# Moving a bias to VectorE, holding fillers behind two norms, and re-timing the gathers of a graph network kernel

## The chip, the cores and the metric

The kernel runs on one core of one Trainium2 chip. A core has five engines that run side by side, each with its own queue of instructions: TensorE (PE in the profile, its weight loads PEld), VectorE (DVE), ScalarE (ACT), GpSimd (POOL) and SyncE (SP, which here only issues DMAs). The metric is the device time of one execution in microseconds; the median of several executions counts.

## The reference

A graph of 2500 nodes with 256 features and 40000 edges goes through two layers, each with a residual. Cut to what matters:

```python
xn = layernorm(x)
x = x + graph_mean(xn) @ W_l.T + xn @ W_r.T + b_r + linear_attention(xn)   # no softmax
x = x + experts(layernorm(x))                    # top 2 of 8, hidden 512
xn = layernorm(x)
x = x + gcn(xn) + transformer(xn)                # 2 aggregations; 4 layers of attention + MLP
x = x + experts1(layernorm(x))                   # shared hidden 1024, best 1 of 8
```

`graph_mean` sums `xn[src]` per `dst` and divides by the count. `gcn` aggregates twice, each time `segment_sum(h[src] * norm, dst) + b` over the edges and a loop on each node, with a leaky rectifier between. One layer of `transformer` is `x += attention(norm(x)); x += gelu(norm(x) @ W1 + b1) @ W2 + b2`, with 256 to 1024 to 256, and attention with a softmax over the features of a query and over the nodes for a key.

## The kernel before

Nodes lie on 125 partitions in 20 tiles (`NT`), worked on in 5 groups (`NG`) of 4 tiles (`GT`, 500 nodes). `X` holds the residual, `Y` the transformer's own. Everything is in fp32, but the one-hots, the adjacency and three bf16 parts of `xn`.

The stages in time: an input stage that finds each node's edges and computes the first attention's 256 x 256 matrix from the Gram matrix of `xn` (to about 81 us); the dense adjacency, built from one-hots, and its product with `xn` (to about 335); the first experts (to about 575); four transformer layers with the two aggregations of `gcn` gathered beside them (to 1711); and the last experts.

*Order.* A framework traces the Python program and plans the order of each engine's instructions by a cost model: an instruction that is planned as ready may be issued ahead of one that stands before it in the program, as a filler. `with tc.issue_after(ins):` keeps what is traced inside it, on the engine of `ins`, behind `ins` in that engine's queue. It adds no wait.

*Input stage.* `norm_stats` (L437 to L440) gives mean and variance, `rsqrt` (L406 to L413) the roots in a dozen small VectorE steps. Groups 0 and 1 are normed first, then 2 to 4; `less` (L756) is the last step of each, and ACT then writes the rows (L763). PE transposes them (L457) and adds up the Gram matrix `pgm` (L769). `count_edges` (L225 to L247) counts edges per node on VectorE and sends the counts through DRAM on SP; `split3` (L447 to L450) splits the rows into three bf16 parts `xb`. Both come after the Gram chain in the program. After them five GpSimd additions put the bias `b0` on `X` (L817), one for each group.

*Adjacency.* `build_tile` makes one-hots `ohd` and `ohs` on VectorE (L151), PE multiplies them (L837), ACT casts the result into `edges` (L840). `neighbours` multiplies `xb` with a group's `edges` (L398); then VectorE adds the two products to `X` (L880, L881). Four tiles are built ahead of the first group.

*Transformer layers.* `attention(l)`: five groups are normed and turned, keys (L1257) follow with their maxima `kmax` (L1259), `top` (L1269, L1270) and the exponentials (L1274); `pk` (L1289) multiplies the transposed keys (L1284, copied by ACT at L1286) with the rows; `context_out` copies it (L1176, L1177). Then come scores of queries by pairs of tiles (`scores`: L1303, L1308 to L1315), their transposes (`turn`: L1321), products (`attend`: L1330) and the addition to `Y` (L1333). `norm_rows(0)` and `norm_turn(0)` norm group 0 for the feed-forward part: `less` (L467), ACT (L469), PE (L457), ACT (L462). `ffn` runs 5 groups with 8 hidden products (L1365, gelu at L1368), 4 times 8 output products (L1376), and an addition (L1378); between them it steps the next groups' attention by a table written by hand.

*Gathers.* The 2000 and more nodes outside group 0 are ranked by degree into 16 ranks of 128. `gathers` fetches for each rank the node's own row and then its neighbours' rows with GpSimd indirect DMAs (L1076), four to a piece, 4 pieces ahead; VectorE adds each piece (L1088; L1092 and L1094 at a rank's end). Round 1 finishes a rank with `rectified` (ACT at L1107 into `b`, VectorE at L1108 to L1111) and scatters it (L1098); round 2 reads that table. Group 0 is multiplied densely instead (`dense`, L1044, finished by `first_group`). Where the adds stand in the program is set by a plan in us: each piece is due at `GATHER` times the gathers before it, counted from the round's beginning, and `conv_step(now)`, called at 88 places of a layer, runs what is due:

```python
while under and under[0][1] + under[0][2] + LANDING <= now:
    run, _, begun = under.pop(0)
    with tc.issue_after(last["add"]):
        passed = next(run, None)
```

`now` is `LAYER * l` plus a share of `AHEAD` in the head of a layer (keys from -0.6 of it, `pk` to 0.7, scores to 0.95), and in `ffn`:

```python
conv_step(LAYER * l + AHEAD + (LAYER - 1.6 * AHEAD) * (g + step / (nj + GT)) / NG)
```

`last["add"]` is the VectorE instruction behind which the adds are queued.

Of the kernel before, what the change touches and what calls it, by code (L numbers as in the profile page):

```python
# [9 lines left out]
F32 = mybir.dt.float32  # L10
# [3 lines left out]
ALU = mybir.AluOpType  # L14
# [4 lines left out]
D = 256  # L19
P = 125  # L20
NT = N // P
GT = 4
NG = NT // GT
# [12 lines left out]
NR = len(MOST)  # L36
SUM = 4
LEAD = 4
GATHER = 1.27
LANDING = 12.0  # L40
LAYER = 237.0
AHEAD = 40.0
NBIN = 64
NE = 8
F0 = 512
# [15 lines left out]
def gps_kernel(ctx: ExitStack, tc: tile.TileContext, a, out):  # L61
# [46 lines left out]
    X = whole[:P]  # L108
# [336 lines left out]
    def split3(dst, src, eng=V):  # L445

        S.copy(dst[:, :, 0, :], src)  # L447
        eng.tensor_tensor(src, src, dst[:, :, 0, :], ALU.subtract)
        S.copy(dst[:, :, 1, :], src)
        eng.tensor_tensor(dst[:, :, 2, :], src, dst[:, :, 1, :], ALU.subtract)  # L450
# [13 lines left out]
    def normal_rows(rows, src, lo, mv, rstd):  # L464

        less = small.tile([P, GT], F32, tag="less", name="less")
        V.scalar_tensor_tensor(less, mv[:, :, 0], -1.0, rstd, ALU.mult, ALU.mult)  # L467
        for k in range(GT):
            S.activation(rows[:, k, :D], src[:, lo + k, :D], AF.Identity, bias=less[:, k:k + 1], scale=rstd[:, k:k + 1])  # L469

    def layernorm_T(src, dst, keep, gain=None, shift=None, stats=None, then=None):

# [254 lines left out]
    with tc.tile_pool(name="lay0", bufs=1) as lay0:  # L727
# [9 lines left out]
        with tc.tile_pool(name="gram", bufs=1) as gram:  # L737
            wk, wv, wfc, wq = (
                load_w(gram.tile([128, 2 * D], F32, name=name[-3:]), a[name], D)
                for name in ("L0_mix_WkT", "L0_mix_WvT", "L0_mix_WfcT", "L0_mix_Wq")  # L740
            )
            bq = gram.tile([128, 2], F32, name="bq")
            nc.sync.dma_start(bq, a["L0_mix_bq"])
            bvc = gram.tile([128, 2], F32, name="bvc")
            nc.sync.dma_start(bvc, a["L0_mix_bv"].rearrange("o (c p) -> p (o c)", p=128))
            bkv = gram.tile([128, 2 * D], F32, name="bkv")
            nc.sync.dma_start(bkv[:, 0:D], row_bcast(a["L0_mix_bk"], 0, D, 128))
            nc.sync.dma_start(bkv[:, D:2 * D], row_bcast(a["L0_mix_bv"], 0, D, 128))


            pgm = [psum2.tile([128, D + 1], F32, tag="ag", name=f"pgm{c}") for c in range(2)]
            rows = []
            for lo, n in ((0, 2 * GT), (2 * GT, NT - 2 * GT)):
                mv, rstd = norm_stats(X, lo, n)
                less = gram.tile([P, n], F32, name="less")
                V.scalar_tensor_tensor(less, mv[:, :, 0], -1.0, rstd, ALU.mult, ALU.mult)  # L756
                for g in range(lo // GT, (lo + n) // GT):
                    t = gram.tile([P, GT, D + 1], F32, tag="t", name="t", bufs=NG)
                    G.memset(t[:, :, D:D + 1], 1.0)
                    rows.append(t)  # L760
                    for k in range(GT):
                        i = g * GT + k
                        S.activation(t[:, k, :D], X[:, i, :D], AF.Identity, bias=less[:, i - lo:i - lo + 1],  # L763
                                     scale=rstd[:, i - lo:i - lo + 1])
                    transpose_group(xT, g, lambda k: t[:, k, :D])
                    for k in range(GT):
                        i = g * GT + k
                        for c in range(2):
                            T.matmul(pgm[c], t[:, k, c * 128:(c + 1) * 128], t[:, k, :], start=(i == 0), stop=(i == NT - 1))  # L769


            gr = gram.tile([128, 2, D + 1], F32, name="gr")
            for c in range(2):
                V.tensor_copy(gr[:, c, :], pgm[c])
            xv = gram.tile([128, 2, D], F32, name="xv")
            for c in range(2):
                ps = mm_tile(128, D)
                for kc in range(2):
                    T.matmul(ps, gr[:, kc, c * 128:(c + 1) * 128], wv[:, kc, :], start=(kc == 0), stop=(kc == 1))
                V.scalar_tensor_tensor(xv[:, c, :], bkv[:, D:2 * D], gr[:, c, D:D + 1], ps, ALU.mult, ALU.add)  # L780
            sv = gram.tile([128, 2], F32, name="sv")
            for c in range(2):
                ps = mm_tile(128, 1)
                for kc in range(2):
                    T.matmul(ps, wv[:, kc, c * 128:(c + 1) * 128], gr[:, kc, D:D + 1], start=(kc == 0), stop=(kc == 1))
                V.scalar_tensor_tensor(sv[:, c:c + 1], bvc[:, c:c + 1], float(N), ps, ALU.mult, ALU.add)
            gm = gram.tile([128, 2, D], F32, name="gm")
            for h in range(2):
                ps = mm_tile(128, 128)
                for kc in range(2):  # L790
                    T.matmul(ps, xv[:, kc, h * 128:(h + 1) * 128], wk[:, kc, h * 128:(h + 1) * 128],
                             start=(kc == 0), stop=(kc == 1))
                cm = gram.tile([128, 128], F32, tag="cm", name="cm", bufs=2)
                V.scalar_tensor_tensor(cm, bkv[:, h * 128:(h + 1) * 128], sv[:, h:h + 1], ps, ALU.mult, ALU.add)
                V.scalar_tensor_tensor(cm, cm, 1.0 / N, heads, ALU.mult, ALU.mult)
                pm = mm_tile(128, D)
                T.matmul(pm, cm, wfc[:, h, :], start=True, stop=True)
                V.tensor_copy(gm[:, h, :], pm)

            for c in range(2):  # L800
                ps = mm_tile(128, D)
                for h in range(2):
                    T.matmul(ps, wq[:, h, c * 128:(c + 1) * 128], gm[:, h, :], start=(h == 0), stop=(h == 1))
                V.tensor_tensor(wx[:, c, :], wx[:, c, :], ps, ALU.add)
            lost = count_edges(gram)
            for g in range(NG):
                split3(xb[:, g * GT:(g + 1) * GT], rows[g][:, :, :D])
            bqs = gram.tile([128, 2, P], F32, name="bqs")
            V.tensor_copy(bqs, bq[:, :, None].to_broadcast([128, 2, P]))
            ps = mm_tile(P, D)  # L810
            for h in range(2):
                T.matmul(ps, bqs[:, h, :], gm[:, h, :], start=(h == 0), stop=(h == 1))
            V.tensor_tensor(b0[:, 0, :], b0[:, 0, :], ps, ALU.add)

        for g in range(NG):
            o = X[:, g * GT:(g + 1) * GT, :D]
            G.tensor_tensor(o, o, b0[:, 0, None, :].to_broadcast([P, GT, D]), ALU.add)  # L817

        degrees(cnt[:, 0:NT])
        rval = small.tile([P, NT], F32, tag="rval", name="rval")  # L820
# [4 lines left out]
        with tc.tile_pool(name="build", bufs=1) as build:  # L825
# [20 lines left out]
            for g in range(NG):  # L846
# [23 lines left out]
                aT = build.tile([128, 2, GC], F32, tag="aT", name="aT", bufs=2)  # L870
                for c in range(2):
                    (S.copy if c else V.tensor_copy)(aT[:, c, :], pa[c])
                for k in range(GT):
                    i = g * GT + k
                    ps = mm_tile(P, 2 * D)
                    for c in range(2):
                        T.matmul(ps[:, :D], xT[:, c, i * P:(i + 1) * P], wx[:, c, :], start=(c == 0), stop=(c == 1))
                    for c in range(2):
                        T.matmul(ps[:, D:], aT[:, c, k * P:(k + 1) * P], wl[:, c, :], start=(c == 0), stop=(c == 1))
                    V.tensor_tensor(X[:, i, :D], X[:, i, :D], ps[:, :D], ALU.add)  # L880
                    V.scalar_tensor_tensor(X[:, i, :D], ps[:, D:], rval[:, i:i + 1], X[:, i, :D], ALU.mult, ALU.add)  # L881
# [107 lines left out]
    with tc.tile_pool(name="big", bufs=4) as big, tc.tile_pool(name="hid", bufs=8) as hid, \  # L989
# [113 lines left out]
        def rectified(o, ps, by, by2):  # L1103

            n = o.shape[0]
            b = conv.tile([128, D], F32, tag="b", name="b")[:n]
            S.activation(b, b1row[:n], AF.Identity, scale=by)  # L1107
            V.scalar_tensor_tensor(o, ps, by2, b, ALU.mult, ALU.add)  # L1108
            neg = conv.tile([128, D], F32, tag="neg", name="neg")[:n]
            V.tensor_scalar(neg, o, 0.0, alpha[:n], ALU.min, ALU.mult)  # L1110
            V.scalar_tensor_tensor(o, o, 0.0, neg, ALU.max, ALU.add)  # L1111
# [103 lines left out]
        def attention(l):  # L1215
# [123 lines left out]

            def norm_rows(g):  # L1340
                mv, rstd = norm_stats(Y, g * GT, GT)
                normal_rows(rows2[:, g * GT:(g + 1) * GT, :], Y, g * GT, mv, rstd)

            def norm_turn(g):
                transpose_group(fT, g, lambda k: rows2[:, g * GT + k, :D], g1[:, 2, :], g1[:, 3, :])
# [43 lines left out]
            def step_scores(u):  # L1389
                qs_of[u] = scores(u)  # L1390
# [7 lines left out]
            for u in range(2):  # L1398
                step_turn(u)
                step_attend(u)  # L1400
            norm_rows(0)
            for u in range(2):
                step_scores(u + 2)
                conv_step(LAYER * l + AHEAD * (0.85 + 0.1 * u))
            norm_turn(0)
            for _ in range(2):
# [316 lines left out]
```

## Time and profile before

| what | value |
|---|---|
| median of 3 runs | 2059.2 us (2053.08 to 2060.47) |
| profiled execution, its own time | 2055.05 us |
| its span, first to last instruction | 2053.4 us |
| mean granted TensorE clock | 0.938 |
| busy: PE, DVE, POOL, ACT | 1777.1, 1006.6, 903.6, 667.8 us |
| indirect DMAs for the gathers (L1076) | 590.7 us busy in its largest group, 1029 ns each |
| adds of pieces (L1088) | 145.9 us busy, 1128 ns each |

A line of the timeline or of a group reads: start and duration in us (in a timeline), engine, source line, operation, what is written and read by the program's names, shapes, the number of instructions merged, and in brackets the engine's idle time before it with what ended it. A line of the waits reads: who waited, for whom, us in total, times, longest. A wait costs time only where the waiting engine is the one that everything else waits for. In the stretches, a pair such as 38.08 (x166) is us busy and instructions, and the clock is a share of full speed.

### The profile page before, as it was taken

The page shows a single profiled execution, that of the slowest core. Times are in us where ns is not written, and L with a number is a line of the kernel's source. Part 1 is how long each engine was busy: PE and PEld are TensorE (multiplying, and loading weights), DVE is VectorE, ACT ScalarE, POOL GpSimd, SP SyncE. Part 2 cuts the span into 40 slices and gives each one's busy share as a digit, 9 for nine tenths or more (in the row PEclk, how much of TensorE's full clock was granted, in tenths as well). Part 3 has the DMA queues.
Part 4 walks back from the last instruction along what each step waited for, and adds up shares of the span by engine and source line. Part 5 has one row for each costly group of instructions (what it writes and reads, how often), then busy time and mean ns, then how long its engine had stood idle before and what let it go on. Part 6 is the DMA issues. An engine that isn't in the chain of part 4 may idle for free. (4 is left out here: it accounts for less than half of the span.)

```text
span 2053.4 us, 24869 instructions
## 1 busy us (share of the span) xinstructions
PE 1777.1 (87%) x8153; PEld 1264.5 (62%) x8153; DVE 1006.6 (49%) x2948; ACT 667.8 (33%) x1228; POOL 903.6 (44%) x898
## 2 busy tenths in 40 slices
PE   2799891999868799997899977998989998976997
PEld 2556551888747567665566655775666766435665
DVE  7867633333362456643567425556444536223333
ACT  1553210322244133442344432434423330442220
POOL 2402632342204567775575575777764310132222
PEclk9799995999979899999999988999999999997999
DMA  5030115675444633373233574456732111511100
GB/s 127 2 98 22 22 29 170 211 234 179 130 128 123 122 80 96 112 206 113 64 96 89 147 131 128 139 154 182 204 109 67 38 41 62 155 38 30 34 21 23
DMA packets 122772, 213.26 MB, mean 104 GB/s; under 512 B 28889, under 2 KB 86881, under 8 KB 122378
## 3 DMA queue, kind: packets, MB, share of 16 engines
q0 software_dynamic: 45632, 105.31, 19.7%
q1 hardware_dynamic: 72181, 98.21, 15.7%
q10 hardware_dynamic: 4821, 8.04, 1.5%
q8 instruction: 70, 1.15, 0.2%
q14 instruction: 68, 0.56, 0.1%
HBM read 172.08 MB, written 41.42 MB: 104 GB/s over the span
## 5 line engine op out<-in xcount | busy, mean ns | idle before, releaser
L1076 POOL DMA_INDIRECT piece<-tab,nbr x574 | 590.7, 1029 | 269.5 <-issue 153.9
L1376 PE MATMUL mm<-w,h 128*125 128x256 f32 x1280 | 290.4, 381 | 5.7 <-ACT h L1368 5.5
L1365 PE MATMUL mm<-xT,w 128*128 128x500 f32 x640 | 290.9, 598 | 2.6 <-ACT xT L462 2.6
L1376 PEld LDWEIGHTS mm<-w,h 128*125 128x125 f32 x1280 | 239.0, 189 | 50.2 <-issue 9.2
L1365 PEld LDWEIGHTS mm<-xT,w 128*128 128x128 f32 x640 | 122.3, 196 | 119.6 <-issue 107.9
L1088 DVE TENSOR_TENSOR piece<-piece 128x1024 f32<-128x1024 f32 (+3 forms) x130 | 145.9, 1128 | 85.8 <-DMA piece<-tab,nbr 85.3
L1368 ACT ACTIVATE h<-mm,bf 128x500 f32<-128x500 f32 x160 | 106.8, 675 | 201.9 <-PE mm L1365 201.7
L398 PE MATMUL pa<-edges,xb 125*128 125x500 bf16 x600 | 137.2, 382 | 1.7 <-ACT edges L840 1.7
L965 POOL DMA_INDIRECT back<-yo,idx x47 | 46.1, 981 | 148.8 <-DVE idx L951 76.6
L1628 PE MATMUL py<-wd,taken 128*128 x432 | 98.6, 386 | 10.4 <-DVE taken L1618 10.4
L457 PE MATMUL mm<-ident,tok 125*128 125x125 f32 x360 | 55.8, 293 | 57.3 <-ACT tok L469 36.4
L945 PE MATMUL mm<-xc,wt 128*128 128x128 f32 x752 | 97.0, 283 | 7.0 <-DVE idx L951 4.2
L521 POOL DMA_INDIRECT sorted<-rows,to x40 | 49.2, 1229 | 121.0 <-DVE to L516 89.4
L1378 DVE TENSOR_TENSOR tok<-tok,mm 125x256 f32<-125x256 f32 x80 | 33.5, 418 | 138.5 <-PE mm L1376 138.4
L945 PEld LDWEIGHTS mm<-xc,wt 128*128 128x128 f32 x752 | 89.8, 195 | 17.1 <-DVE xc L941 11.6
L959 PE MATMUL py<-w,h 128*128 x376 | 97.7, 386 | 2.1 <-ACT h L949 2.0
L1333 DVE TENSOR_TENSOR tok<-tok,po 125x256 f32<-125x256 f32 x80 | 30.0, 417 | 141.3 <-PE po L1330 141.2
L398 PEld LDWEIGHTS <-xb 125*128 125x128 bf16 x600 | 58.8, 101 | 65.3 <-issue 6.8
L1628 PEld LDWEIGHTS py<-wd,taken 128*128 128x128 f32 x432 | 82.5, 193 | 25.9 <-DVE taken L1618 13.4
L949 ACT ACTIVATE h<-mm,wt 128x128 f32<-128x128 f32 x188 | 53.7, 368 | 136.7 <-issue 127.3
L1289 PE MATMUL pk<-kt,tok 125*128 125x256 f32 x320 | 80.3, 402 | 18.4 <-ACT kt L1286 16.8
L840 ACT CAST edges<-mm 125x500 bf16<-125x500 f32 x100 | 64.6, 783 | 82.9 <-PE mm L837 82.9
(407 smaller groups left out, 3041.5 us busy)
## 6 DMA issues: line engine op xcount, KB each, us to landing
wt<-in_expert_in_dram SPq DMA_DIRECT2D x47, 514.0 KB
sorted<-nothing SPq DMA_DIRECT2D x5, 2031.2 KB
piece<-tab,nbr POOLq DMA_INDIRECT x574, 3.1
e<-adj SPq DMA_DIRECT2D x40, 218.8 KB
w<-in_L_mix_W_dram SPq DMA_DIRECT2D x8, 1024.0 KB
wd<-in_L_ffn_Wd_dram SPq DMA_DIRECT2D x8, 1024.0 KB
xs<-sorted SPq DMA_DIRECT2D x47, 130.0 KB
t<-tab SPq DMA_DIRECT2D x20, 224.0 KB
```

The source lines that it names most:

```text
L398: T.matmul(pa[c], table[:, k, n, c * 128:(c + 1) * 128], edges[:, k, :], start=(k == 0 and n == 0), stop=(k == NT - 1 and n == 2))
L457: T.transpose(ps[:, k * P:(k + 1) * P], src_of(k)[:, c * 128:(c + 1) * 128], ident[:P, :P])
L840: S.copy(o.rearrange("p s (n d) -> p n s d", d=BD), ps[:P].rearrange("p (n s d) -> p n s d", n=BD, d=BD))
L945: T.matmul(ps[:, j * TS:(j + 1) * TS], wt[:, c * F0 + j * 128:c * F0 + (j + 1) * 128], xc[:, c * TS:(c + 1) * TS], start=(c == 0), stop=(c ...
L959: T.matmul(ps, h[:, j * TS:(j + 1) * TS], w2[:, ds(e, 1), j, :], start=(j == 0), stop=(j == NJ - 1))
L1076: G.indirect_dma_start(out=t[:, i, :], out_offset=None, in_=tab, in_offset=bass.IndirectOffsetOnAxis(ap=by, axis=0))
L1088: V.tensor_tensor(total[:, :m, :], total[:, :m, :], t[:, :m, :], ALU.add)
L1289: T.matmul(pk[c], rows[:, i, c * 128:(c + 1) * 128], kt, start=(i == 0), stop=(i == NT - 1))
L1365: T.matmul(ps, w1[:, c, j * 128:(j + 1) * 128], fT[:, c, g * GC:(g + 1) * GC], start=(c == 0), stop=(c == 1))
L1368: S.activation(h, ps, AF.Gelu, bias=bf[:, l, j:j + 1])
L1376: last["product"] = T.matmul(ps, hh[j][:, k * P:(k + 1) * P], w2[:, j, :], start=(j == 0), stop=(j == nj - 1)).ins
L1628: T.matmul(ps, h[:, j * TS:(j + 1) * TS], wd[:, ds(e, 1), j, :], start=(j == 0), stop=(j == nj - 1))
```

## The change

Five edits. The first layer's bias is added on VectorE, for one group at a time, inside the loop over groups, just before the products of that group are added. `count_edges` and `split3` are queued, on VectorE, behind the `less` of the second norm (the loop's variable `normed` holds the last one). `normal_rows` and `norm_rows` return their `less`; the scores of the second two pairs, and the gather adds traced there, are queued on VectorE behind it. `b` of `rectified` gets two buffers. And the plan's constants become 1.38 us a gather, 270 us a layer and 57 us for a layer's head.

```diff
-GATHER = 1.27
+GATHER = 1.38
-LAYER = 237.0
-AHEAD = 40.0
+LAYER = 270.0
+AHEAD = 57.0
...
     def normal_rows(rows, src, lo, mv, rstd):
-        V.scalar_tensor_tensor(less, mv[:, :, 0], -1.0, rstd, ALU.mult, ALU.mult)
+        made = V.scalar_tensor_tensor(less, mv[:, :, 0], -1.0, rstd, ALU.mult, ALU.mult)
...
+        return made.ins
...
-                V.scalar_tensor_tensor(less, mv[:, :, 0], -1.0, rstd, ALU.mult, ALU.mult)
+                normed = V.scalar_tensor_tensor(less, mv[:, :, 0], -1.0, rstd, ALU.mult, ALU.mult)
...
-            lost = count_edges(gram)
-            for g in range(NG):
-                split3(xb[:, g * GT:(g + 1) * GT], rows[g][:, :, :D])
+            with tc.issue_after(normed.ins):
+                lost = count_edges(gram)
+                for g in range(NG):
+                    split3(xb[:, g * GT:(g + 1) * GT], rows[g][:, :, :D])
...
-        for g in range(NG):
-            o = X[:, g * GT:(g + 1) * GT, :D]
-            G.tensor_tensor(o, o, b0[:, 0, None, :].to_broadcast([P, GT, D]), ALU.add)
...
                     (S.copy if c else V.tensor_copy)(aT[:, c, :], pa[c])
+                o = X[:, g * GT:(g + 1) * GT, :D]
+                V.tensor_tensor(o, o, b0[:, 0, None, :].to_broadcast([P, GT, D]), ALU.add)
...
-            b = conv.tile([128, D], F32, tag="b", name="b")[:n]
+            b = conv.tile([128, D], F32, tag="b", name="b", bufs=2)[:n]
...
-                normal_rows(rows2[:, g * GT:(g + 1) * GT, :], Y, g * GT, mv, rstd)
+                return normal_rows(rows2[:, g * GT:(g + 1) * GT, :], Y, g * GT, mv, rstd)
...
-            norm_rows(0)
+            last["add"] = norm_rows(0)
             for u in range(2):
-                step_scores(u + 2)
+                with tc.issue_after(last["add"]):
+                    step_scores(u + 2)
                 conv_step(LAYER * l + AHEAD * (0.85 + 0.1 * u))
```

## The prediction

> **What bounds the kernel now.** I read the page first, for how much TensorE (PE) leaves over.
>
> ```profile
> span 2053.4 us, 24869 instructions
> ...
> PE 1777.1 (87%) x8153; PEld 1264.5 (62%) x8153; DVE 1006.6 (49%) x2948; ACT 667.8 (33%) x1228; POOL 903.6 (44%) x898
> ...
> PE   2799891999868799997899977998989998976997
> ...
> PEclk9799995999979899999999988999999999997999
> ```
>
> PE is the busiest, so time is won only where PE idles or runs at a low clock: the first slices, and low digits between 700 and 1711 us, where the four attention layers run. The busy times by stretch (columns: PE, PEld, DVE, ACT, POOL, clock, DMA share, GB/s) show the head of layer 1, with both PE and the clock down to nine tenths or less:
>
> ```profile
> 900.00:950.00 50.00, 38.08 (x166) 28.71 (x165) 16.41 (x27) 19.09 (x46) 38.73 (x38) 0.90 0.46 132
> 950.00:1000.00 50.00, 37.87 (x167) 28.62 (x166) 25.54 (x70) 15.66 (x29) 18.30 (x20) 0.90 0.28 85
> ```
>
> The waits of 700 to 1720 us name the engines in front of PE:
>
> ```profile
> DVE piece L1088 <- DMA piece<-tab,nbr: 69.3, 12, 15.0
> ...
> ACT tok L469 <- DVE less L467: 50.5, 24, 9.7
> ...
> PE mm L457 <- ACT tok L469: 36.4, 13, 9.5
> ...
> ACT b L1107 <- DVE sums L1108: 27.9, 13, 8.1
> ```
>
> Two things: VectorE (DVE) stands at adds of gathered rows that have not landed, and PE waits for a normalisation whose roots are late. The timeline of layer 1 shows the latter:
>
> ```profile
> 977.31 0.75 DVE L1333 TENSOR_TENSOR tok<-tok,po 125x256 f32<-125x256 f32 x2 [1.45 <-PE po L1330]
> ...
> 983.48 1.23 DVE L1088 TENSOR_TENSOR piece<-piece 128x1024 f32<-128x1024 f32 x1
> ...
> 987.38 0.16 DVE L467 SCALAR_TENSOR_TENSOR less<-mv,rstd 125x4 f32<-125x4 f32 x1
> ...
> 988.23 2.16 PE L457 MATMUL mm<-ident,tok 125*128 125x125 f32 x8 [8.37 <-ACT tok L469]
> ```
>
> Between the last input (978.1) and its result (987.5) DVE was never idle: it ran scores and gather adds between the small steps of the root. The gathers' own stalls, in the heads of layers 1 and 2:
>
> ```profile
> 930.22 0.51 ACT L1107 ACTIVATE b<-b1row,disr 128x256 f32<-128x256 f32 x1 [8.06 <-DVE sums L1108]
> ...
> 935.62 3.78 PE L1289 MATMUL pk<-kt,tok 125*128 125x256 f32 x8 [11.68 <-ACT kt L1286]
> ```
>
> ```profile
> 1201.88 1.23 DVE L1088 TENSOR_TENSOR piece<-piece 128x1024 f32<-128x1024 f32 x1 [7.56 <-DMA piece<-tab,nbr]
> ...
> 1205.61 1.22 PE L1284 MATMUL mm<-ident,xT 128*125 128x128 f32 x4 [12.23 <-ACT xT L1274]
> ```
>
> Last, the timeline of the first 110 us: the roots of the second norm take from 39.05 to 51.22, and five bias additions on GpSimd (POOL) lie beside the one-hots that PE needs.
>
> ```profile
> 39.05 0.17 DVE L440 TENSOR_SCALAR var<-mv 125x12 f32<-125x12 f32 x1
> ...
> 51.22 0.16 DVE L756 SCALAR_TENSOR_TENSOR less<-mv,rstd 125x12 f32<-125x12 f32 x1
> ```
>
> ```profile
> 83.55 17.44 POOL L817 TENSOR_TENSOR X<-X,b 125x1024 f32<-125x1024 f32 x5
> 83.85 3.98 DVE L151 TENSOR_TENSOR ohs<-kth,slo 128x3200 bf16<-128x3200 bf16 x1
> ...
> 95.30 2.27 PE L837 MATMUL mm<-ohd,ohs 128*128 128x100 bf16 x25 [5.15 <-DVE ohs L151]
> ...
> 107.87 1.81 DVE L151 TENSOR_TENSOR ohs<-kth,slo 128x3200 bf16<-128x3200 bf16 x1
> ```
>
> **Part 1, the bias.** Five POOL additions go (17.44 us in a row); while they run, a one-hot takes 3.6 to 4.0 us, against 1.45 and 1.81 without them. At full speed ACT becomes the limit there: its first ten casts (L840) end at 87.5, ten more at 3.24 per five end at 94.0, against 99.2 in the trace: 5.1 us won. Added are five DVE additions, priced by the nearest row (L1357, same shape, 1227 ns): 6.1 us. If the planner puts them into DVE's waits of 2 to 3.3 us between the one-hots of 105 to 131 us, they cost nothing; put before the fourth tile's one-hots, where I count 1.2 us of room, they cost 4.9. I take 1.1. Net 4, ends 0 and 5.
>
> **Part 2, counting and splitting behind the roots.** From `var` to `less` is 12.2 us; the same dozen dependent steps unmixed (141.1 to 143.4 in the trace) take 2.4. ACT could normalise from about 43, when its first casts are done, instead of 51.85: 9 us earlier. But the pushed work is not gone: four compares and four reductions of 0.82, ten split steps of 1.22, small ones, together 20 us of DVE, and DVE is busy 36.8 of the 43 us from 38 to 81. So at most its 6.2 us of idle time can be won, and `edges` cannot be written before the splitting ends, since it takes that memory. The counts' two DMAs and `byrow` on SP move some 10 us back; SP has nothing behind them before 104.6, but PE's transpose of `byrow` (67.0) stands ahead of the Gram products and could hold them a few us. I take 4.5, ends -6 and 6.
>
> **Part 3, scores behind a layer's norm.** From 978.1: two statistics (0.75), two aggregates (0.3), twelve steps of 0.2, then ACT's first row (0.65): PE could start at 982.2, not 988.2. The four gaps are 6.4, 8.4, 9.5 and 8.0, in all 32.3; in layer 0 nothing should stay (PE is busy to 703.2), in the others 2.3 each: 25.4 won. After each gap the next L1365 run at half speed (six in 4.23 us at 991; elsewhere eight in 3.35), some 2 us a layer. A gap of 2.29 us at 968.6 was followed by nearly full speed (eight L1330 in 1.99, else 1.73), so I add 4.5: 30. The delayed scores (about 6 us of DVE and two ACT exponentials for two pairs) are needed by PE's transposes (L1321) only after the second hidden product, some 7 us later; gather adds queue behind them, not ahead. If that cover is gone, PE waits up to 1.5 us a layer. Ends 14 and 38. No DMA moves here.
>
> **Part 4, the gathers' clock.** The planned times are proportions of a layer, so they must be set against its real length: the first L1365 of the layers start at 712.4, 991.0, 1269.9 and 1538.8, so 279, 279 and 269 us, where the kernel says 237; the new 270 fits. The head (keys to first hidden product) is really about 84 us without its stalls (106 from 884 to 990, less 11.7, 8.4 and 2); the old numbers give 59, the new 84; the feed-forward is 170 to 175, old 173, new 179. So the old plan asks 1.27 us a gather in the feed-forward, while POOL at its densest makes 38 in 50 us, 1.316: DVE then waits at the adds. The new plan asks 1.38 of 270, 1.34 in the feed-forward. A round is 303 gathers and 16 steps, so round 1 needs 12 + 319 x 1.38 = 452 of the plan's us and ends seven tenths into layer 1's feed-forward, earlier than before (at four fifths); round 2's first adds come 23 later, and hand-over (7.8 in the trace, 1136.75 to 1144.5), ten us of gathers and a landing of 3 need 21. In the old plan the margin grew by 0.08 us a piece, now by 0.5.
>
> What this frees: PE's gap of 12.2 at 1193 (DVE behind two landings, then `kmax` and `top`), the 5.5 at 1429, two of about 1 at 844 and 1124, and about 2 of low clock, less 4 us that I leave for landings of up to 12.5 us while weights and `sorted` load: 17.7. The second buffer of `b` frees ACT from the 8 us before 930.22, behind which the copies of `kt` queued; the gap is 11.7 and 2 of clock, but the next `b` stood right behind it, so I take two thirds, 9. Sum 26.7, ends -10 and 36. The plan's adds in the product of keys (L1289) go to a DVE that has nothing else there until the copy at 959 (idle 23.8): no cost.
>
> One rule speaks against this part. Row: the 95 gathers issued beside an add take 1.32 us on average, the others 0.98. SBUF - State Buffer, section "Who interferes with whom", says that a DVE instruction with two SBUF inputs contends with a GpSimd one that reads SBUF, and section "SBUF: two separate sides" that the loser blocks for the whole instruction. Each add (1.22) is such a one: four gathers at 1.25 and one add in full make 6.2, or 1.555 a gather, an estimate by that page; then the plan runs ahead by 0.21 a step, some 135 us of DVE waits over 638 steps. Before, 69 us of these waits made about 29 of PE gaps; so 135 make about 57 and part 4 is -26 instead of +26.7. I take the row: 1.316 already holds these delays.
>
> **Sum.** 4 + 4.5 + 30 + 26.7 = 65 off 2055.05 us (the profiled execution, 2053.4 of it span): 1990. That execution lies 4.2 under the median of 2059.2, so I say 1994 for the median.
>
> **Rivals.** A (0.78): as summed. B (0.14), gathers as the page's rule has them, or adds that the planner clumps anyway: parts 1 to 3 alone, 38, with part 4 between 0 and -26: 2021 to 2047, middle 2034. For it: a shorter layer (279 less some 24) makes 1.38 worth 1.30, just under 1.316. Against: a stall lengthens the layer and heals itself. C (0.04): the planner orders much as before; the stalls stay, only part 1's 4 us come: 2055. D (0.04), slower: gathers become the limit, DVE standing in order at each add in the keys and feed-forward. With a step of p us, waits are 638 x (p - 1.34), 0.43 of them PE gaps, against 38 from the other parts and 31 of such gaps that exist now; it turns above p = 1.59, and at 1.65 gives about 2075. Against it: no dense stretch is over 1.32.
>
> **How the numbers follow.** No change is within 0.5%, 10 us, about what a measurement of this kernel can tell. A is faster throughout; half of C and little of B is the same; D is slower, with some of C for orders of the planner that I can't see: faster 0.92, same 0.04, slower 0.04. All parts at their good ends give 1974 (85 off); A with half its unknowns failing gives 2020; B's middle is 2034. The range is 1970 to 2034.
>
> **What would show it.** Right: no POOL additions near 83, one-hots of 1.5 to 1.8 from the start, `less` (L756's second) near 43; the gap before L457 at each layer's norm under 3 us; L1088's waits below 25 us and none ahead of `top`; first L1365 of the layers some 255 us apart. Wrong: a build start still near 81, L1321 waiting on scores, waits at L1088 growing along round 2, or the low clock still after each norm.

## The result, and the profile after

The changed kernel takes 2068.8 us (median of 8 runs, 2065.6 to 2075.3) against 2058.7 for the kernel before on the same chip: a ratio of 1.0051, 95% interval [1.0035, 1.0067]. It is 10 us slower; the forecast was 65 us faster. The profiled execution took 2070.42 us.

The page of the changed kernel. TensorE does the same 8153 instructions at the same mean clock (0.938). Of the 14.7 us by which this span is longer than the one profiled before, 8 are TensorE's busy time and 7 its idle time:

```profile
span 2068.1 us, 24880 instructions
...
PE 1785.0 (86%) x8153; PEld 1265.7 (61%) x8153; DVE 1009.8 (49%) x2953; ACT 667.4 (32%) x1228; POOL 886.4 (43%) x893
...
PE   2899892999787699994899878999999999985997
...
PEclk9799995999888899997999999999999999997999
```

The waits of 700 to 1720 us, the window shown of before (who, for whom, us in total, times, longest). The norm's wait in front of PE fell from 36.4 to 10.1. The adds' waits rose from 69.3 to 99.0, and ScalarE's at `b` doubled:

```profile
DVE piece L1088 <- DMA piece<-tab,nbr: 99.0, 23, 12.7
...
ACT b L1107 <- DVE sums L1108: 53.9, 10, 28.5
...
PE pk L1289 <- ACT kt L1286: 27.6, 1, 27.6
...
PE mm L457 <- ACT tok L469: 10.1, 13, 2.5
```

The timeline of layer 1's norm: twelve steps of 0.16 to 0.17 us in a row, with nothing between them, and a gap of 2.35 in place of 8.37.

```profile
1005.25 0.17 DVE L440 TENSOR_SCALAR var<-mv 125x4 f32<-125x4 f32 x1
...
1007.63 0.16 DVE L467 SCALAR_TENSOR_TENSOR less<-mv,rstd 125x4 f32<-125x4 f32 x1
1007.71 1.28 DVE L1308 TENSOR_REDUCE qm<-mm 125x16 f32<-125x512 f32 x2
...
1008.48 1.81 PE L457 MATMUL mm<-ident,tok 125*128 125x125 f32 x7 [2.35 <-ACT tok L469]
```

The loss lies in the products of keys. In layer 0, VectorE does five adds where it did two, each but the first some 4 us behind the last one, when its gathers land, and the copy `fk` that TensorE needs stands behind them in the same queue. The timelines of VectorE alone, first of before:

```profile
649.65 1.23 DVE L1088 TENSOR_TENSOR piece<-piece 128x1024 f32<-128x1024 f32 x1 [12.06 <-DMA piece<-tab,nbr]
654.82 1.23 DVE L1088 TENSOR_TENSOR piece<-piece 128x1024 f32<-128x1024 f32 x1 [3.95 <-DMA piece<-tab,nbr]
663.59 0.42 DVE L1177 COPY fk<-pk 128x256 f32<-128x256 f32 x1 [7.55 <-PE pk L1289]
```

```profile
645.90 1.23 DVE L1088 TENSOR_TENSOR piece<-piece 128x1024 f32<-128x1024 f32 x1 [11.70 <-DMA piece<-tab,nbr]
651.18 1.22 DVE L1088 TENSOR_TENSOR piece<-piece 128x1024 f32<-128x1024 f32 x1 [4.06 <-DMA piece<-tab,nbr]
656.49 1.23 DVE L1088 TENSOR_TENSOR piece<-piece 128x1024 f32<-128x1024 f32 x1 [4.09 <-DMA piece<-tab,nbr]
661.71 1.23 DVE L1088 TENSOR_TENSOR piece<-piece 128x1024 f32<-128x1024 f32 x1 [3.99 <-DMA piece<-tab,nbr]
666.90 1.23 DVE L1088 TENSOR_TENSOR piece<-piece 128x1024 f32<-128x1024 f32 x1 [3.96 <-DMA piece<-tab,nbr]
668.04 0.42 DVE L1177 COPY fk<-pk 128x256 f32<-128x256 f32 x1
```

PE's next product (L1182) starts at 668.51 after a gap of 8.11. The dense product's loads then come late as well: PE waits 7.7 and 7.3 us for `e<-adj` (L1044), 2.6 and 2.9 before. The stretch from the first L1289 to the first L1365 of layer 0 is 87.5 us, 74.9 before. In layer 1 the same reaches PE through ScalarE:

```profile
938.95 3.09 DVE L1088 TENSOR_TENSOR piece<-piece 128x1024 f32<-128x1024 f32 x3 [10.37 <-DMA piece<-tab,nbr]
...
950.54 1.22 DVE L1088 TENSOR_TENSOR piece<-piece 128x1024 f32<-128x1024 f32 x1 [8.50 <-DMA piece<-tab,nbr]
...
958.51 0.51 ACT L1107 ACTIVATE b<-b1row,dis 125x256 f32<-125x256 f32 x1 [28.54 <-DVE sums L1108]
...
958.93 0.35 ACT L1286 COPY kt<-mm 125x256 f32<-125x256 f32 x1
...
959.34 3.28 PE L1289 MATMUL pk<-kt,tok 125*128 125x256 f32 x6 [27.58 <-ACT kt L1286]
```

VectorE waits for gathers; ScalarE's sum of bias waits for a buffer that VectorE frees; the copies `kt` stand behind that sum; TensorE waits 27.58 us for a copy of 0.35.

### The profile page after: what moved, and what is told of

The parts are those of the page before. It is cut to its first block, busy times and chain, and to the rows that moved or that the text cites. A ratio compares the mean times of both kernels' runs of the same rounds, so it can differ in the third digit from the quotient of the medians.

```text
span 2068.1 us, 24880 instructions
## 1 busy us (share of the span) xinstructions
PE 1785.0 (86%) x8153; PEld 1265.7 (61%) x8153; DVE 1009.8 (49%) x2953; ACT 667.4 (32%) x1228; POOL 886.4 (43%) x893
## 3 DMA queue, kind: packets, MB, share of 16 engines
q8 instruction: 70, 1.15, 0.2%
## 4 chain that ended last, share of the span: by engine, by line
PE 33%; issue 17%; POOL 11%; DVE 9%; DMA 9%; ACT 2%; SPq 0%; DVEq 0%; POOLq 0%; ACTq 0%
PE mm L1376 8%; POOL piece L1076 7%; PE mm L1365 7%; DMA piece<-tab,nbr 4%; PE mm L1257 3%; PE mm L945 2%; PE py L959 2%; PE po L1330 2%; PE mm L1303 2%; DVE piece L1088 2%; PE mm L457 1%; PE mm L1487 1%; POOL out_dram L1638 1%; DVE st L437 1%; ACT tok L469 1%
## 5 line engine op out<-in xcount | busy, mean ns | idle before, releaser
L1365 PE MATMUL mm<-xT,w 128*128 128x500 f32 x640 | 293.1, 601 | 8.3 <-ACT h L1368 5.2
L1088 DVE TENSOR_TENSOR piece<-piece 128x1024 f32<-128x1024 f32 (+3 forms) x130 | 146.8, 1132 | 127.2 <-DMA piece<-tab,nbr 126.8
L1365 PEld LDWEIGHTS mm<-xT,w 128*128 128x128 f32 x640 | 122.4, 196 | 125.9 <-issue 108.9
L398 PE MATMUL pa<-edges,xb 125*128 125x500 bf16 x600 | 136.5, 380 | 1.9 <-ACT edges L838 1.9
L1289 PE MATMUL pk<-kt,tok 125*128 125x256 f32 x320 | 81.0, 403 | 34.2 <-ACT kt L1286 32.7
L1378 DVE TENSOR_TENSOR tok<-tok,mm 125x256 f32<-125x256 f32 x80 | 33.6, 420 | 147.7 <-PE mm L1376 147.5
L398 PEld LDWEIGHTS <-xb 125*128 125x128 bf16 x600 | 58.6, 101 | 65.1 <-issue 6.3
L1333 DVE TENSOR_TENSOR tok<-tok,po 125x256 f32<-125x256 f32 x80 | 30.1, 417 | 131.5 <-PE po L1330 131.5
L1044 PE MATMUL da<-t,e 125*125 125x256 f32 x320 | 81.2, 395 | 15.1 <-DMA e<-adj 15.1
L469 ACT ACTIVATE tok<-tok,less,rstd 125x256 f32<-125x256 f32 x140 | 72.8, 593 | 60.7 <-DVE less L467 59.9
```

The lines of the kernel that those rows point to most:

```text
L398: T.matmul(pa[c], table[:, k, n, c * 128:(c + 1) * 128], edges[:, k, :], start=(k == 0 and n == 0), stop=(k == NT - 1 and n == 2))
L1044: T.matmul(sums[d // 2][:, d % 2, :], e[:, d * P:(d + 1) * P], t[:, k, :], start=(i + k == 0 and d % 2 == 0), stop=(i + k == NT - 1 and d ...
L1088: V.tensor_tensor(total[:, :m, :], total[:, :m, :], t[:, :m, :], ALU.add)
L1289: T.matmul(pk[c], rows[:, i, c * 128:(c + 1) * 128], kt, start=(i == 0), stop=(i == NT - 1))
L1365: T.matmul(ps, w1[:, c, j * 128:(j + 1) * 128], fT[:, c, g * GC:(g + 1) * GC], start=(c == 0), stop=(c == 1))
```

## The experiments

There were five series, each compared with the kernel before on its own chip. Two chips took 2057 to 2060 us for that kernel, as the first did; three took 2305 to 2323 (the last section says what was seen there). So ratios are compared, and the sizes are taken from the first kind.

**The parts apart.** Bias, counting and splitting alone; the scores alone; the constants alone; and the changed kernel with the old constants.

```diff
 # e3_clock: the kernel before with these; e4_oldclock and g1_oldclock: the changed kernel without
-GATHER, LAYER, AHEAD = 1.27, 237.0, 40.0
+GATHER, LAYER, AHEAD = 1.38, 270.0, 57.0
```

> Before, with the first layer's bias on VectorE and the counting and splitting behind the roots; nothing else. By the prediction's steps 8.5 us less (4 and 4.5). By the trace of the changed kernel, where the first experts start 3.3 us earlier, about 3 us less. Rival: the later count pushes other work back, 0 or some us more; then the front shares in the loss.

> Before, with the scores behind the norm alone. My theory: this part did what was forecast and its gain is eaten by the sums' clock, so alone it gives 25 to 30 us less, with the gaps ahead of L457 at the norms at none in layer 0 and about 2.5 in the others. Rival: pushing the scores back delays the matmuls of the scores as much as the norm gains, so that this part is the loss: then 0 to 10 us more.

> Before, with the three constants of the sums' clock (1.38, 270, 57) and nothing else. My theory: with them the planner puts more adds into the products of keys, where they stand in VectorE's queue ahead of the copies and sums that TensorE waits for; 25 to 40 us more than before. The prediction's step: 17.7 us less. Rival: the constants are harmless and another part (b's second buffer, scores, front) is the loss: within 5 us of before.

> The changed kernel with the three old constants (1.27, 237, 40); bias, count, scores and b's second buffer stay. My theory: the sum of the other parts is left, 25 to 38 us less than before. Rival (b's second buffer, the scores or the front are the loss): about as slow as the changed kernel, 5 to 15 us more than before.

Measured, on a chip at 2304.8 us: e1_front 0.9978 [0.9949, 1.0008], unclear; e2_scores 0.9919 [0.9892, 0.9947]; e3_clock 1.0214 [1.0163, 1.0265]; e4_oldclock 0.9902 [0.9864, 0.9940]. The constants alone lose 2%, the rest gains 1%. The rival "the constants are harmless" is out. The scores alone gave 19 us (12 to 25), less than the 25 to 30 expected, though the gaps at the norms went as forecast (none, then 2.35, 2.35 and 2.34; 6.41, 8.37, 9.54 and 8.02 in e1_front, which leaves the scores as they were). e1_front is compatible with anything from 12 us less to 2 more.

> The changed kernel with the three old constants (1.27, 237, 40), once more, on a chip whose layers may be quicker: its first run fell on one on which the kernel before took 2304.8 us. My theory: 25 to 38 us less than before. Rival (b's second buffer, the scores or the front are the loss): as slow as the changed kernel, 5 to 15 us more than before.

On a chip at 2059.9 us: 2025.3 us, 0.9839 [0.9815, 0.9863]. The other parts are worth 33 us; against this, the constants of the changed kernel (1.0051) cost some 44.

**The second buffer of `b`.**

```diff
 # e4_oldclock with
-            b = conv.tile([128, D], F32, tag="b", name="b", bufs=2)[:n]
+            b = conv.tile([128, D], F32, tag="b", name="b")[:n]
```

> The changed kernel with the old constants and one buffer of `b` as before. By the prediction's step the second buffer is worth 9 us, so 2034 us. By the trace of the run with the old constants and two buffers, where the gap of 11.7 us in the second layer's product of keys is still 10.7, it is worth 1 to 3: 2026 to 2028.

> The changed kernel with the old constants and one buffer of `b`, once more, for a chip on which the kernel before takes about 2059 us. By the prediction's step the second buffer is worth 9 us: 2034. By the trace of the run with two buffers it is worth 1 to 3: 2026 to 2028.

h3_oneb 0.9894 [0.9850, 0.9938] at 2315.8 us; j3_oneb, at 2056.5, 2021.2 us and 0.9841 [0.9819, 0.9863]. With two buffers it was 0.9839: nothing that can be measured, not 9 us.

**Which queue carries the loss to TensorE.** Three kernels from the changed one: own buffers for the four dense groups; six buffers for all; no adds inside the product of keys.

```diff
 # f1_b0: in first_group, rectified(..., tag="b0"); i1_six and j2_six: bufs=6
 # f2_hold:
-                conv_step(LAYER * l + AHEAD * i / NT * 0.7)
...
-                V.scalar_tensor_tensor(gm[:, h, :], ps[:, :D], rows_by[:, h:h + 1], gm[:, h, :], ALU.mult, ALU.add)
+                last["add"] = V.scalar_tensor_tensor(gm[:, h, :], ps[:, :D], rows_by[:, h:h + 1], gm[:, h, :], ALU.mult, ALU.add).ins
```

> The changed kernel, with the four `b` of the first group of nodes under a tag of their own, so that ScalarE's sum of a dense group no longer waits for a buffer that stands behind the gathered sums. My theory: the gap of 27.6 us in the second layer's product of keys shrinks by 10 to 20 us, and with it the time: 0 to 10 us less than before, 10 to 20 us less than the changed kernel. Rival: VectorE, where the adds stand, keeps the copies waiting anyway; then within 4 us of the changed kernel.

> The changed kernel with six buffers of `b` for two, so that ScalarE never stands at a sum of bias that waits for VectorE. My theory: the copies `kt` of the second layer's product of keys no longer stand behind it, and TensorE makes the product while VectorE waits for gathers; the gap of 27.6 us shrinks to under 8, and the time falls by 15 to 25 us to 2045 to 2055. Rival: VectorE's copy `fk` behind the same adds holds TensorE as long; within 5 us of 2070.

> The changed kernel with six buffers of `b` once more, for a chip on which the kernel before takes about 2059 us. My theory: TensorE makes the second layer's product of keys while VectorE waits for gathers; the gap of 27.6 us there shrinks to under 8, and the time falls to 2045 to 2058. Rival: the copy `fk`, behind the same adds, holds TensorE as long; within 5 us of 2070.

f1_b0 1.0060 [1.0041, 1.0079], j2_six 1.0076 [1.0054, 1.0098], i1_six (at 2315.8 us) 1.0128 [1.0083, 1.0172]. My expectation failed: the gap stays. The timeline of j2_six in layer 1:

```profile
962.06 0.51 ACT L1107 ACTIVATE b<-b1row,disr 128x256 f32<-128x256 f32 x1 [28.82 <-DVE sums L1108]
...
962.48 0.35 ACT L1286 COPY kt<-mm 125x256 f32<-125x256 f32 x1
...
962.88 1.65 PE L1289 MATMUL pk<-kt,tok 125*128 125x256 f32 x3 [27.86 <-ACT kt L1286]
```

With six buffers more sums are made ahead, and the next one waits for the same L1108 as before: ScalarE's next `b` is queued as soon as the plan counts a buffer as free, so it always stands at the newest add.

> The changed kernel, with no add handed out in the loop of the product of keys; those that are due follow behind the last sum of the context's matrices. My theory: the adds ahead of the copy `fk` are the loss; the gaps ahead of it (8.1 us in layer 0, 27.6 in layer 1, 3.1 in layer 2) go, and the time is 15 to 30 us less than the changed kernel, 5 to 20 us less than before. Rival: the adds stand ahead of the scores' work instead and TensorE waits there; within 5 us of the changed kernel.

f2_hold gave 1.0059 [1.0036, 1.0081], as slow as the changed kernel. All three gaps ahead of `fk` and in the products of keys did go (layer 0's stretch from L1289 to L1365 is 58.4 us, not 87.5), but the adds went ahead of the scores' steps, and PE waits there, the rival's case. Timeline, layer 1:

```profile
931.83 5.22 DVE L1088 TENSOR_TENSOR piece<-piece 128x1024 f32<-128x1024 f32 x5
...
941.57 1.23 DVE L1088 TENSOR_TENSOR piece<-piece 128x1024 f32<-128x1024 f32 x1 [3.27 <-DMA piece<-tab,nbr]
...
950.46 1.10 PE L1321 MATMUL mm<-ident,q 125*128 125x125 f32 x4 [15.21 <-DVE q L1315]
```

So neither queue alone is the cause. Where the adds that are due too early stand in the queues only decides whom they hold up.

**Which constant, and which way.** All from the changed kernel, with these values:

```diff
-GATHER, LAYER, AHEAD = 1.38, 270.0, 57.0
+GATHER, LAYER, AHEAD = 1.38, 270.0, 40.0    # f3_ahead40
+GATHER, LAYER, AHEAD = 1.27, 270.0, 46.0    # h2_quick
+GATHER, LAYER, AHEAD = 1.38, 237.0, 40.0    # h1_slow, j1_slow
+GATHER, LAYER, AHEAD = 1.46, 237.0, 40.0    # k1_slower
```

> The changed kernel with AHEAD at its old 40, LAYER 270 and GATHER 1.38 kept. My theory: AHEAD is what moves more of the adds into the heads of the layers, so that most of the loss goes: 15 to 35 us less than the changed kernel. Rival: LAYER and GATHER do it; then within 5 us of the changed kernel.

> The changed kernel with GATHER 1.38 and the old LAYER 237 and AHEAD 40. Counted in real time, at layers of about 272 us, the plan then hands out one gather's share in 1.58 us (the old constants 1.46, the changed ones 1.39, and POOL delivered one in 1.42 to 1.51 us in the two rounds seen so far, once 1.34). My theory: adds that are planned ahead of their gathers are the loss, so a slower plan is no slower than the old constants' 2025 us, 2005 to 2025; VectorE's waits for gathers fall under 70 us, and the adds end near 1670, just ahead of the end of the layers. Rival: a slower plan puts the last adds behind the layers, 10 to 30 us more than with the old constants (2035 to 2055).

> The changed kernel with GATHER 1.27, LAYER 270 and AHEAD 46: the share of the heads as in the kernel before (AHEAD is 0.17 of LAYER), and a plan of 1.28 us for one gather in real time, quicker than POOL delivers. My theory: VectorE's waits for gathers grow to over 130 us, spread over heads and hidden products, and the time is 10 to 40 us more than the changed kernel's 2070. Rival: the heads' share is what counts; then it is as quick as the old constants, 2025 to 2040.

> GATHER 1.38 with the old LAYER and AHEAD once more (a plan of 1.58 us for one gather in real time), for a chip on which the kernel before takes about 2059 us; on one that took 2316 us it gave 0.980 of before. My theory (the plan has to stay behind the gathers): 2005 to 2025 us, no slower than the old constants' 2025, with VectorE's waits for gathers under 70 us. Rival: here POOL isn't held back by the other engines, the last adds land behind the layers and the time is 2035 to 2055.

> GATHER 1.46 with the old LAYER and AHEAD: a plan of 1.68 us for one gather in real time; its 638 steps fill 4.0 layers, so that the last adds come due at the end of the layers. By the prediction's rival D the gathers become the limit from 1.59 us on: 15 to 40 us more than with GATHER 1.38. Rival: the last adds fit beside the last hidden products, within 5 us of GATHER 1.38.

At 2315.8 us: h1_slow 0.9798 [0.9753, 0.9843], h2_quick 1.0208 [1.0161, 1.0254]. On the quicker kind: f3_ahead40 1.0073 [1.0045, 1.0101]; j1_slow 1996.3 us, 0.9719 [0.9701, 0.9737]; k1_slower 2021.5 us, 0.9835 [0.9816, 0.9853]. AHEAD is not it (f3_ahead40 against the changed kernel), against my expectation. One constant at a time: GATHER from 1.27 to 1.38 takes 1.2% off (g1_oldclock to j1_slow), LAYER from 237 to 270 puts 3.5% on (j1_slow to f3_ahead40), AHEAD does nothing that can be measured at LAYER 270.

Two readings fit these runs. The first takes the plan as a whole: GATHER / LAYER is the share of a layer that it leaves for one gather. That was 5.36 thousandths before; the change made it 5.11, so the plan as a whole became 5% quicker although GATHER went up. The ratios below follow this share, with the best near 5.8; h2_quick, at 4.70, was the slowest of its series.

The second takes the time that the plan leaves for one gather stretch by stretch. The product of keys gets 0.7 x AHEAD / GATHER gathers and takes 23.2 us from its first matmul to its last where nothing disturbs it (layers 2 and 3); the feed-forward part gets (LAYER - 1.6 x AHEAD) / GATHER and takes 171 (696.3 to 866.9 in j1_slow). POOL's steps of under 2 us are 1.25 us at the median and 1.30 to 1.31 in the mean, in all of these kernels. The waits are those of 630 to 1690 us, adds for gathers and gathers for adds:

| kernel | share of a layer, thousandths | keys, us a gather | feed-forward | adds wait | gathers wait | ratio |
|---|---|---|---|---|---|---|
| f3_ahead40 | 5.11 | 1.14 | 1.15 | 99.1 | 76.7 | 1.007 |
| changed kernel | 5.11 | 0.80 | 1.32 | 126.8 | 54.7 | 1.005 |
| g1_oldclock | 5.36 | 1.05 | 1.26 | 81.3 | 66.9 | 0.984 |
| j1_slow | 5.82 | 1.14 | 1.36 | 60.3 | 93.6 | 0.972 |
| k1_slower | 6.16 | 1.21 | 1.44 | 39.7 | 140.6 | 0.984 |

The stretches tell where the waits fall. How long they are in all, the share alone would tell as well: the changed kernel and f3_ahead40 have the same share and, within the noise, the same time. No run here separates the two readings further.

The changed kernel asks too much of the heads. f3_ahead40 asks too much of the feed-forward parts, and the new gaps are there (9.9, 11.6 and 12.4 us at 853, 1154 and 1437); the second in its timeline, where the late add stands ahead of a norm's roots, the norm ahead of a gelu on ScalarE, and TensorE behind the gelu:

```profile
1159.55 1.29 DVE L1088 TENSOR_TENSOR piece<-piece 128x1024 f32<-128x1024 f32 x1 [6.00 <-DMA piece<-tab,nbr]
...
1163.20 1.58 ACT L469 ACTIVATE tok<-tok,less,rstd 125x256 f32<-125x256 f32 x3 [15.28 <-DVE less L467]
...
1164.69 0.65 ACT L1368 ACTIVATE h<-mm,bf 128x500 f32<-128x500 f32 x1
...
1165.39 1.22 PE L1376 MATMUL mm<-w,h 128*125 128x256 f32 x2 [11.55 <-ACT h L1368]
```

j1_slow leaves POOL more than it needs in the long stretches, and more often it is the gathers that wait for the adds; that pieces then lie ready for the short stretches is what I take from this. Its page, with PE doing the same work in 21 us less than in the changed kernel, at a mean clock of 0.953:

```profile
span 1987.3 us, 24876 instructions
...
PE 1764.2 (89%) x8153; PEld 1257.4 (63%) x8153; DVE 1010.4 (51%) x2953; ACT 666.3 (34%) x1228; POOL 886.6 (45%) x893
...
PEclk9799996899979999998999999999999999988999
```

k1_slower is the far end: adds wait least, but the last ones come after the layers, where the next transposes need them:

```profile
1672.67 0.96 DVE L1088 TENSOR_TENSOR piece<-piece 128x768 f32<-128x768 f32 x1 [1.82 <-DMA piece<-tab,nbr]
...
1674.49 0.68 DVE L1156 TENSOR_TENSOR tok<-da,dval 125x512 f32<-125x512 f32 x1
...
1675.23 2.03 PE L457 MATMUL mm<-ident,tok 125*128 125x125 f32 x8 [9.98 <-DVE tok L1156]
```

That is some 14 of the 25 us by which it is slower than j1_slow (9.98 here and 4.5 at 1682); its layers also end 18 us later, which I have not taken apart.

**The sum of bias on VectorE**, to take the wait off ScalarE's queue; from j1_slow (m1_slow_dve) and from the changed kernel (m2_dve):

```diff
-            S.activation(b, b1row[:n], AF.Identity, scale=by)
+            V.tensor_scalar(b, b1row[:n], by, None, ALU.mult)
```

> GATHER 1.38 with the old LAYER and AHEAD, and the sum's bias `b` made on VectorE instead of ScalarE, so that ScalarE's queue has no instruction that waits for the gathered sums. My theory: the gap of 8.4 us that is left in the second layer's product of keys goes, for some 48 more instructions of about 0.3 us on a VectorE that has room; 0.967 to 0.971 of before, 3 to 8 us less than with GATHER 1.38 alone (0.972). Rival: the 15 us more on VectorE stand ahead of copies that TensorE waits for, or the copy `fk` waits there instead: 0.970 to 0.976.

> The changed kernel with `b` made on VectorE instead of ScalarE. More buffers of `b` took nothing off ScalarE's wait of 28.5 us, since ScalarE asks for each buffer as soon as it is free; this takes the instruction itself out of ScalarE's queue. My theory: the copies `kt` pass, TensorE makes the second layer's product while VectorE waits, and what is left of the gap of 27.6 us stands ahead of `fk` with under 10; 12 to 22 us less than the changed kernel's 1.005 to 1.008 of before, so 0.994 to 1.001. Rival: VectorE's adds hold `fk` as long as they held ScalarE: 1.003 to 1.010.

At 2322.7 us: 0.9832 [0.9794, 0.9869] and 1.0152 [1.0111, 1.0193]. On such chips h1_slow gave 0.9798 and the changed kernel was not run, so this shows no gain and settles nothing: there the product of keys of layer 0 takes 70 and 81 us in these two (25 on the quicker kind). Whether it helps on the quicker kind stays open.

## Why the prediction was wrong, step by step

- **Part 1 (4 us): right.** In the changed kernel the one-hots take 1.46 and 1.82 us from the start, and from the first cast to the first L398 it is 12.6 us, against 18.0 before (83.30 to 95.89, and 81.22 to 99.23): 5.4 won, 5.1 forecast before what was taken off for the VectorE additions. The first experts start 3.3 us earlier, as the adjacency does, so these additions cost nothing that shows.

- **Part 2 (4.5 us): wrong, nothing won.** `less` was to come near 43; it came at 51.37 (51.22 before). The counting and splitting did move behind it, and the planner put other fillers in their place: four one-hots of the adjacency (1.46 and 1.82 us) between `var` and `less`. Two of them in VectorE's timeline:

```profile
43.30 0.17 DVE L406 TENSOR_SCALAR half<-var 125x12 int32<-125x12 int32 x1
43.38 1.82 DVE L151 TENSOR_TENSOR ohs<-kth,slo 128x3200 bf16<-128x3200 bf16 x1
...
47.83 0.17 DVE L411 TENSOR_TENSOR y<-y 125x12 f32<-125x12 f32 x1
47.91 1.82 DVE L151 TENSOR_TENSOR ohs<-kth,slo 128x3200 bf16<-128x3200 bf16 x1
49.65 0.17 DVE L412 SCALAR_TENSOR_TENSOR y<-y,var 125x12 f32<-125x12 f32 x1
```

  The step that failed is "ACT could normalise from about 43": holding two fillers back frees the place for a third. The casts start at 83.30, against 81.22 before; but e2_scores and e3_clock, which have the old input stage, start them at 83.49 and 84.15, so a loss isn't shown either. Together parts 1 and 2 gave 3 to 6 us, not 8.5 (the first L398 at 96.0 on average in nine profiles of kernels with both on the quicker kind of chip; 99.2 before, 101.5 and 102.2 in those two).

- **Part 3 (30 us): right in the gaps, wrong in the clock.** The four gaps were 32.3 us and are 7.4 (none, 2.35, 2.51, 2.50): 24.9 won, 25.4 forecast; no L1321 waits longer for its scores than the 2.2 us at 993.5. The 4.5 us for the low clock behind the gaps came in layer 0 alone, where no gap is left: the first eight L1365 take 3.62 us, 6.16 before. Behind the gaps of 2.4 us of layers 1 to 3 they take 6.54, 6.29 and 6.68 us (5.07, 5.56 and 5.94 before). Layer 1, before and changed; the granted clock, as a share of full speed, is 0.67 from 990 to 996 in the first and 0.50 from 1010.5 to 1016.5 in the second:

```profile
991.04 5.07 PE L1365 MATMUL mm<-xT,w 128*128 128x500 f32 x8 [0.65 <-ACT xT L462]
```

```profile
1011.15 6.54 PE L1365 MATMUL mm<-xT,w 128*128 128x500 f32 x8 [0.72 <-ACT xT L462]
```

  So the one gap of 2.29 us with nearly full speed behind it, on which the 4.5 rested, did not speak for these; and "the low clock still after each norm", named as a sign of being wrong, was there.

- **Part 4, the second buffer (9 us): wrong, 0.** The text saw that "the next `b` stood right behind it" and still took two thirds. The six buffers show that this was the whole answer.

- **Part 4, the constants (17.7 us): wrong, -44.** Three steps failed. "The plan's adds in the product of keys (L1289) go to a DVE that has nothing else there until the copy at 959 (idle 23.8): no cost": those adds are 29 gathers in a loop of 23 us, and wait past it, with `fk` and `b` behind them. And the head was taken as one stretch of 84 us with the right sum, though the plan spreads it by fixed shares: the longer AHEAD went to the one part that had no time for it. And "the new 270 fits" looked at LAYER alone: in a layer of 279 us the old plan left 279 x 1.27 / 237 = 1.50 us for a gather, the new one 279 x 1.38 / 270 = 1.43. The text saw that round 1 would end "earlier than before", and took it for harmless. Its margin of 0.5 us a piece sets the plan's 1.38 against POOL's 1.25; by its own 1.34 and 1.316 it would have been 0.1. The feed-forward rate was right (1.34 forecast, 1.32 by its real length); no gap of the changed kernel lies in the feed-forward parts but one of 5.2 at 1169, where round 2 begins.

- **The rivals.** B named it ("adds that the planner clumps anyway") but bounded it at -26 and gave it 0.14. Its other reason was the rule that an add blocks a gather in full, from which 1.555 us a gather was estimated by the Trainium skill's page SBUF - State Buffer, sections "Who interferes with whom" and "SBUF: two separate sides". The rule is seen in the trace; the estimate is not. A gather that POOL begins while an add runs ends 0.82 us after the end of that add (0.818 to 0.823 for eight in ten of the 75 in the changed kernel that had more than 0.15 us of it left), where one by itself takes 0.95:

```profile
839.12 1.22 DVE L1088 TENSOR_TENSOR piece<-piece 128x1024 f32<-128x1024 f32 x1
839.21 1.94 POOL L1076 DMA_INDIRECT piece<-tab,nbr  x1 [0.30 <-issue]
...
841.46 0.95 POOL L1076 DMA_INDIRECT piece<-tab,nbr  x1 [0.30 <-issue]
```

  Beside a VectorE instruction that has an input in PSUM (L1310, L1333, L1378) gathers take 0.95 as well. But the estimate charged every add in full, 0.3 us a gather. In the changed kernel 90 of the 118 adds of 0.9 us and more met a gather, and it had some 0.4 us of the add to wait for: 37 us over 606 gathers, or 0.06 each. So taking the row was right. "A stall lengthens the layer and heals itself", held against B, was wrong: the layers grew to 289.5 and 283.8 us, and the heads' bursts stayed. D's 2075 us lies near the 2069 measured by luck: it needed a step above 1.59 us.

- **The sum.** Parts 1 to 3 without the second buffer, 38.5 forecast, gave 35 (j3_oneb, 2056.5 to 2021.2). In part that is luck: 3 to 6 from the front, 24.9 from the gaps and 2.5 from the clock of layer 0 make 30 to 33, and the gap of 12.2 us behind `top`, which part 4 was to free, is 7.7 there. The constants turned a gain of 17.7 into a loss of 44. j1_slow comes out 60 us below the kernel before on its chip, where 65 was forecast: GATHER alone, with LAYER and AHEAD left, won the 25 us that part 4 was to bring. Of the gaps that part 4 named, those of 12.2 and 5.5 us are gone in it, and 8.4 is left of 11.7.

## What to carry to other kernels

Work that is dealt out by a plan beside a bound engine must be compared with its supplier twice: over the whole period, where a longer time for each item gives the supplier nothing if the period that it is counted in is stretched still more; and stretch by stretch, at the length each stretch really has. Here the plan asked a stretch of 23 us for 29 transfers that take 1.25 us each, and an add that waits holds all that stands behind it in its queue, and what waits for that in the next. Leave the supplier more time than it needs, and test the plan on both sides of the best value. Where a filler is held back to shorten a chain, look for what takes its place; a gap that is made shorter need not spare the clock behind it (half the clock after 2.35 us here); and another buffer doesn't take a wait away if its next user is queued as soon as it is free.

## What had not been expected of the hardware

Three of the five chips ran the kernel before in 2305 to 2323 us. Up to 580 us, and after the layers, their profiles agree with the others to a few us; the loss lies where the gathers run. The mean granted clock of the profiled executions was 0.886 to 0.904 there and 0.933 to 0.953 on the others; which of the two brings the other is not known. There TensorE stood still with no wait that the profile shows (`issue`); in the same window no profile of the quicker kind has such a line for it. Waits of e4_oldclock, whose kernel ran as g1_oldclock on the other kind (630 to 1990 us):

```profile
PE pk L1289 <- issue: 70.0, 13, 14.0
PE mm L457 <- issue: 19.5, 10, 11.5
```

POOL's step was the same, 1.25 us at the median, and the adds waited less for gathers (18.1 us). What holds the engines there was not found. The versions came in the same order on both kinds: GATHER 1.38 alone (h1_slow), the old constants (h3_oneb, e4_oldclock), and the changed constants (i1_six).
